# A graph-attention kernel: tiles of x transposed by VectorE in 32x32 blocks, with the features in another order, in place of TensorE

## The chip, the cores and the metric

The kernel runs on one core of a Trainium2 chip. The metric is the device time of one execution in microseconds (us). Timed runs are given as their median; the profile is of one further execution, whose own time is given beside it.

## The reference

There are N = 3327 nodes with D = 512 features, an N x N matrix `adj` of zeros and ones, two weight matrices of 512 x 1024 (one per attention layer) and one of 512 x 512. All is float32.

```
for l in 0, 1:                       # two attention layers
    Wh, Ws = split(x @ W[l])         # each N x 512
    a = softmax(Wh @ Ws.T) * adj     # N x N
    x = leaky_relu(a @ Wh + x)
x = layernorm(x0 + x)
b = max(sign(x), 0)
x = layernorm(x + relu(adj @ (b @ sign(weight).T)))
```

The order of the 512 features is free inside one product that sums over them, as long as both sides use the same order. The change rests on that.

## The kernel before

Rows of x are cut into tiles of 128 (26 tiles, the last with 127 rows), four tiles make a chunk (7 chunks, the last with two tiles), two tiles make a pair. Each layer has two stages: `project`, then `attention`.

**project(l)** makes what attention reads. Its matmuls sum over the features, so the features must lie on the partitions: each chunk of x is needed as `xT`, 128 feature partitions x 4 feature blocks x 512 rows. `load_x(c)` loads the chunk's tiles `xr` by rows (one DMA of 256 KB a tile, on SP's queue). `transpose_x(c, k, lane)` transposes the four tiles' block k on TensorE through PSUM, four instructions (L263), and copies the result to `xT` with one copy by ACT (L268; for chunk 0 by ACT and VectorE in turn, L121 and L123).

From `xT` come three things:

- `keys`: four sums of quarter blocks of `xT` on VectorE (L180 to L183), all stored to DRAM (`xs_d`) by POOL's queue.
- `project_values`: Wh of a pair as a product of Strassen's form, `seven`: seven products (`pZ_wh`, `pX_wh`, `pY_wh`) of the quarters of `xT` with those of `wa` (the first half of W) and with `wsum`, sums of those quarters made by `sums_w` on VectorE. Three PSUM banks, X, Y and Z, hold partial sums. A product that adds to bank Z must wait until ACT has copied out what was there (L159).
- `queries`: the chunk's x times M, in the same form (`pZ_g`, `pX_g`, `pY_g`), where M is the product of the two halves of W (`product_m`, tiles `pm`, matmuls L235). M needs both halves transposed, which `transpose_w` does on TensorE (L213, copies `wTs`). `xt` are sums of quarters of `xT` (L186 to L189), `msum` sums of quarters of M.

In layer 0, M is made at the beginning of `project`. In layer 1 it is made during the last steps of the first attention: `load_w` loads both halves on SP's queue, `transpose_w` and `product_m` are woven between attention's matmuls.

**attention(l)** goes through 13 x 13 steps. SP's queue brings `ws`, `adj`, `xs` and `gs` a few steps ahead; VectorE and ACT make the softmax, POOL sums, TensorE the products of scores and of values. Rows of the next x are finished by VectorE (L790, L793) and stored to `x1_d`.

The order of instructions on each engine is written out by hand: `weave` sorts pieces of several lists by their place in the list, and pieces like the transposes of the next chunk (`turns`) stand between the matmuls of the current one. All small tiles come from one ring of equal slots (`slot`). After layer 1's begin, `binary_weights` loads four tiles `wT` through a ring of two buffers and works on them on VectorE (L464, L466).

Of the kernel before, what the change touches and what calls it, by code (L numbers as in the profile page):

```python
# [19 lines left out]
P = 128  # L20
CT = 4
CW = CT * P
HW = CW // 2
NEG_SLOPE = 0.01
EPS = 1e-5
# [4 lines left out]
def kernel(  # L30
# [21 lines left out]
    def tiles_of(c):  # L52
        return range(c * CT, min(NT, (c + 1) * CT))
# [23 lines left out]
    def slot(shape, dtype, name):  # L77
        return ring.tile(shape, dtype, tag="s", bufs=SBUFS, name=name)
# [32 lines left out]
    def load_rows(eng, dst, src, r):  # L111

        cut = r - r % 16
        if cut:
            eng.dma_start(out=dst[:cut], in_=src[:cut])
        if cut < r:
            eng.dma_start(out=dst[cut:r], in_=src[cut:r])

    def copy_out(n, dst, src):
        if n % 2:  # L120
            nc.scalar.copy(dst, src)  # L121
        else:
            nc.vector.tensor_copy(dst, src)  # L123
# [76 lines left out]
    ch_lane, acc_lane, tr_lane = (ps_ch, "ch"), (ps_acc, "acc"), (ps_tr, "tr")  # L200
    w_rows, wT, m_of, wsum_of = {}, {}, {}, {}

    def load_w(l, h):

        for k in range(KD):
            w_rows[l, h, k] = slot([P, D], F32, f"w{h}_{l}_{k}")
            nc.sync.dma_start(out=w_rows[l, h, k], in_=w_stack[l, ts(k, P), ts(h, D)])

    def transpose_w(l, h, k, lane):
        pool, tag = lane  # L210
# [32 lines left out]
    def project(l, pre):  # L243
# [1 line left out]
        src = x if l == 0 else x1_d  # L245
        xTs, rows_of = {}, {}

        def load_x(c):
            rows_of[c] = []
            for t in tiles_of(c):  # L250
                xt = slot([P, D], F32, f"xr_{l}_{t}")
                load_rows(nc.sync, xt, src[t * P : t * P + rows(t), :], rows(t))
                rows_of[c].append(xt)

        def transpose_x(c, k, lane):
            if k == 0:
                xTs[c] = pre.tile([P, KD, CW], F32, tag="xT", bufs=2, name=f"xT_{l}_{c}")
            pool, tag = lane
            pt = pool.tile([P, CW], F32, tag=tag, name=f"pxt_{l}_{c}_{k}")
            w = 0  # L260
            for a, t in enumerate(tiles_of(c)):
                r = rows(t)
                nc.tensor.transpose(  # L263
                    pt[:, w : w + r], rows_of[c][a][:r, ts(k, P)], ident[:r, :r]
                )
                w += r
            if c:
                nc.scalar.copy(xTs[c][:, k, :w], pt[:, :w])  # L268
            else:
                copy_out(k, xTs[c][:, k, :w], pt[:, :w])  # L270
            n = len(tiles_of(c)) * P
            if w < n:
                nc.gpsimd.memset(xTs[c][:, k, w:n], 0.0)


        load_x(0)
        wa = pre.tile([P, KD, D], F32, tag="wa", bufs=1, name=f"wa_{l}")
        for k in range(KD):
            nc.sync.dma_start(out=wa[:, k], in_=w_stack[l, ts(k, P), :D])
        if l == 0:  # L280
            load_w(l, 1)
            for k in range(KD):
                w_rows[l, 0, k] = wa[:, k]
        load_x(1)
        for k in range(KD):
            transpose_x(0, k, acc_lane)
        if l == 0:
            for h in range(2):
                for k in range(KD):
                    transpose_w(l, h, k, (acc_lane, ch_lane)[h])  # L290
        if l == 0:
            for k in range(2):
                sums_w(l, k)
        wsum = wsum_of[l]
        lo, hi = wa[:, 0:2], wa[:, 2:4]
        wr = {B11: lo[:, :, :HD], B21: hi[:, :, :HD], B22: hi[:, :, HD:]}
        wr.update({i: wsum[:, e] for e, i in enumerate((T1, T2, T3, T4))})
        m = pre.tile([P, KD, D], F32, tag="m", bufs=1, name=f"m_{l}")
        if l == 0:
            m_of[l] = [m[:, 0:2], m[:, 2:4]]  # L300
# [120 lines left out]
        def prepare(c):  # L421
            start, *chains[c] = queries(c, (ch_lane, ch_lane if c else acc_lane))
            if start:
                start()

        if l == 0:
            first, second = (project_values(0, a, ch_lane) for a in range(2))
            weave(product_m(l, acc_lane), first + second, [lambda: prepare(0)])
            sums_m()
        else:  # L430
            first, second = (
                project_values(0, a, lane) for a, lane in enumerate((ch_lane, acc_lane))
            )
            weave(first, second, [sums_m, lambda: prepare(0)])
        for c in range(NC):
            turns = []
            if c + 1 < NC:
                turns = [lambda k=k: transpose_x(c + 1, k, tr_lane) for k in range(KD)]
                pairs_of[c + 1] = project_values(c + 1, 0, acc_lane)
                turns += [pairs_of[c + 1].pop(0), lambda: prepare(c + 1)]  # L440
            turns = rest + turns
            rest = [chains[c][1].pop()] if chains[c][1] else []
            if c + 2 < NC:
                load_x(c + 2)
            if c == 0:
                weave(*chains[c], turns)
            else:
                one, two = chains[c]
                pairs = pairs_of[c]
                for a in range(1, len(tiles_of(c)) // 2):  # L450
                    pairs += project_values(c, a, acc_lane)
                rest.append(pairs.pop())
                weave(one + two, pairs, turns)
# [735 lines left out]
```

## Time and profile before

| | us |
|---|---|
| three timed runs | 2652.05, 2652.95, 2653.69 |
| median | 2652.95 |
| profiled execution, its own time | 2652.55 |
| its span, first to last instruction | 2650.7 |
| TensorE busy | 2614.6 |
| VectorE busy | 2046.3 |
| ACT busy | 812.1 |
| POOL busy | 1091.3 |
| mean share of the 16 DMA engines on SP's queue | 60.4% |

PE is TensorE's matmuls and PEld its weight loads, which overlap them; DVE is VectorE, ACT ScalarE, POOL GpSimd, SP SyncE, and SPq the DMAs that SP issues. A name such as `pxt<-ident,xr` gives the tile written and the tiles read; xN is a count. Matmuls overlap, so that the duration of one is longer than the distance to the next: what a matmul costs TensorE is read from the starts. A float32 product appears as two rows per matmul of the source. In rows in order of time, the first number is the start in us from the span's begin, the second the time from there to the end of the last instruction merged into the row, and the brackets give the idle time before it and what ended it.

### The profile page before, as it was taken

To read this page: it belongs to the slowest core of one execution; us is meant where nothing else is said; L and a number is where in the kernel's file an instruction comes from. 1 tells how busy PE (TensorE), PEld (TensorE's weight loads), DVE (VectorE), ACT (ScalarE), POOL (GpSimd) and SP (SyncE) were. 2 spreads that over 40 slices of the span, in tenths; PEclk is the share of its full clock that TensorE was granted. 3 is DMA by queue.
4 is the path that set the end of the run, shared out by engine and by line. 5 is a ranking of instruction groups with operands and counts; after the bars stand their busy time and mean duration, and the time that the engine had idled before them with its cause. 6 is when DMAs were issued, how large, how long until landed. Compare 5 with 4: busy or idle time off the path is not lost. (4 is left out here: it accounts for less than half of the span.)

```text
span 2650.7 us, 40451 instructions
## 1 busy us (share of the span) xinstructions
PE 2614.6 (99%) x12839; PEld 2271.0 (86%) x12864; DVE 2046.3 (77%) x4211; ACT 812.1 (31%) x2000; POOL 1091.3 (41%) x2029
## 2 busy tenths in 40 slices
PE   9999999999999999999999999999999999999998
PEld 7888888888888888887888888888888888888787
DVE  5554888899888896666754589988899888767976
ACT  3333332333333332221333333333333333222143
POOL 2550343444444444546552044444444444455510
PEclk9999999999999999999999999999999999999999
DMA  5754777777777776776865677777777777677875
GB/s 205 272 193 157 260 239 251 253 266 252 259 244 244 267 248 222 235 245 230 294 219 180 210 231 272 241 257 260 233 270 247 252 255 236 228 260 260 278 245 168
DMA packets 285186, 638.63 MB, mean 241 GB/s; under 512 B 32141, under 2 KB 146671, under 8 KB 283430
## 3 DMA queue, kind: packets, MB, share of 16 engines
q1 hardware_dynamic: 249206, 529.52, 60.4%
q0 software_dynamic: 35760, 106.45, 10.8%
q8 instruction: 105, 1.72, 0.3%
q14 instruction: 115, 0.94, 0.1%
HBM read 528.91 MB, written 106.93 MB: 240 GB/s over the span
## 5 line engine op out<-in xcount | busy, mean ns | idle before, releaser
L500 PE MATMUL pZ<-gs,xs 128*128 128x256 f32 x2496 | 636.2, 379 | 1.7 <-ACT u L517 1.7
L699 POOL TENSOR_TENSOR as<-s 128x128 f32<-128x128 f32 x338 | 163.4, 484 | 1037.0 <-DVE s L661 691.9
L500 PEld LDWEIGHTS pZ<-gs,xs 128*128 128x128 f32 x2496 | 473.3, 190 | 67.8 <-ACT u L517 3.6
L726 PE MATMUL acc<-ws,s 128*128 128x256 f32 x1352 | 402.6, 379 | 0.0
L726 PE MATMUL acc<-wh,s 128*128 128x256 f32 x1352 | 355.9, 379 | 0.0
L726 PE MATMUL acc<-ws,as 128*128 128x256 f32 x1352 | 349.7, 380 | 1.8 <-POOL as L701 1.2
L648 ACT ACTIVATE s<-s 128x512 f32<-128x512 f32 x338 | 213.3, 631 | 377.7 <-DVE s L645 377.1
L500 PE MATMUL pY<-gs,xs 128*128 128x256 f32 x1248 | 320.7, 379 | 2.2 <-ACT p L517 2.2
L726 PEld LDWEIGHTS acc<-ws,as 128*128 128x128 f32 x1352 | 255.2, 190 | 42.3 <-issue 5.8
L726 PEld LDWEIGHTS acc<-wh,s 128*128 128x128 f32 x1352 | 257.3, 190 | 35.2
L726 PEld LDWEIGHTS acc<-ws,s 128*128 128x128 f32 x1352 | 256.2, 190 | 34.4
L570 DVE TENSOR_TENSOR top<-top,s 128x512 f32<-128x512 f32 x312 | 225.4, 735 | 69.0 <-ACT s L557 48.5
L500 PEld LDWEIGHTS pY<-gs,xs 128*128 128x128 f32 x1248 | 236.7, 190 | 36.0 <-ACT p L517 3.8
L645 DVE TENSOR_TENSOR s<-s,off 128x512 f32<-128x512 f32 x338 | 249.2, 737 | 0.1
L661 DVE TENSOR_TENSOR s<-s,adj 128x512 f32<-128x512 f32 x338 | 236.8, 701 | 9.4 <-DMA adj<-in_adjT_dram 1.0
L656 DVE TENSOR_TENSOR total<-total,s 128x512 f32<-128x512 f32 x312 | 231.8, 743 | 0.0
L517 ACT COPY u<-pZ 128x256 f32<-128x256 f32 x312 | 115.8, 371 | 345.5 <-PE pZ L500 344.9
L701 POOL TENSOR_TENSOR as<-s 128x128 f32<-128x128 f32 x338 | 204.7, 606 | 26.5
L726 PE MATMUL acc<-wh,as 128*128 128x256 f32 x676 | 203.0, 382 | 0.0
L700 POOL TENSOR_TENSOR s<-s 128x128 f32<-128x128 f32 x338 | 183.3, 542 | 27.6
L702 POOL TENSOR_TENSOR as<-s,as 128x128 f32<-128x128 f32 x338 | 180.7, 535 | 26.5
L542 DVE TENSOR_TENSOR s<-p,u 128x256 f32<-128x256 f32 x156 | 66.8, 428 | 151.7 <-ACT u L517 151.7
(206 smaller groups left out, 3883.9 us busy)
## 6 DMA issues: line engine op xcount, KB each, us to landing
ws<-ws_d SPq DMA_DIRECT2D x338, 512.0 KB, 3.8
xs<-xs_d SPq DMA_DIRECT2D x182, 512.0 KB, 5.8
adj<-in_adjT_dram SPq DMA_DIRECT2D x324, 256.0 KB, 4.2
xs<-xs_d SPq DMA_DIRECT2D x156, 384.0 KB, 6.5
gs_d<-gsp POOLq DMA_DIRECT2D x88, 256.0 KB, 2.8
gs<-gs_d SPq DMA_DIRECT2D x12, 1792.0 KB, 10.9
adj_d<-ab POOLq DMA_DIRECT2D x169, 112.0 KB, 3.8
ahl<-adj_d SPq DMA_DIRECT2D x78, 224.0 KB, 4.7
```

Of the source, the lines that this page charges most:

```text
L500: nc.tensor.matmul(ch[bank], xs[c, q, a][:, k], gs[c][:, b, k], start=(start and k == 0), stop=(k == 1), skip_group_check=True,)
L517: nc.scalar.copy(ch[name], ch[bank])
L570: nc.vector.tensor_tensor(top[i], top[i], t, ALU.max)
L645: nc.vector.tensor_tensor(s, s, off[g].to_broadcast([P, 2, HW]), ALU.subtract)
L648: nc.scalar.activation(sc[g, q], sc[g, q], AF.Exp)
L656: nc.vector.tensor_tensor(total[g], total[g], sc[g, q], ALU.add)
L661: nc.vector.tensor_tensor(s, s, adj[g, q], ALU.mult)
L699: nc.gpsimd.tensor_tensor(s3, a11, a21, ALU.subtract)
L700: nc.gpsimd.tensor_tensor(a21, a21, a22, ALU.add)
L701: nc.gpsimd.tensor_tensor(s2, a21, a11, ALU.subtract)
L702: nc.gpsimd.tensor_tensor(s4, a12, s2, ALU.subtract)
L726: nc.tensor.matmul(acc[g][i // 2][:, i % 2], a[i], b[i], start=(q == 0 and i % 2 == 0), stop=(q == NQ - 1), skip_group_check=True,)
```

## The change

`load_x` now loads one tile so that its four 128-column blocks lie on four quadrants of 32 partitions: one DMA for each quadrant (`load_laid`), in which partition v of the quadrant gets row v of each of the tile's four groups of 32 rows. `transpose_x` is then one VectorE instruction a tile, which transposes every 32x32 block. No PSUM tile and no copy remain. After it, partition 32a+u of block k holds feature 128a+32k+u, so the rows of both halves of W are loaded in that order too: `load_features` (four DMAs for `wa`, as before) and `load_w` (16 DMAs for a half, before 4). At the begin of each layer's `project`, the DMAs are issued by SP and ACT in turn; everywhere else by SP. The begin is in another order: the first pair's product starts when two tiles and `wa` are there, and the transposes of W follow, woven between its products.

```diff
--- before.py
+++ after.py
@@ -20,6 +20,7 @@
 P = 128
 CT = 4
 CW = CT * P
+B = 32
 HW = CW // 2
 NEG_SLOPE = 0.01
 EPS = 1e-5
@@ -116,6 +117,36 @@
         if cut < r:
             eng.dma_start(out=dst[cut:r], in_=src[cut:r])
+    def load_laid(engines, dst, src, n):
+        full = n // B
+        for a in range(CT):
+            eng = engines[a % len(engines)]
+            if full:
+                eng.dma_start(
+                    out=dst[ts(a, B), :full],
+                    in_=src[: full * B, ts(a, P)].rearrange("(r v) f -> v r f", v=B),
+                )
+            if full * B < n:
+                cut = (n - full * B) // 16 * 16
+                for lo, hi in ((0, cut), (cut, n - full * B)):
+                    if lo < hi:
+                        eng.dma_start(
+                            out=dst[a * B + lo : a * B + hi, full],
+                            in_=src[full * B + lo : full * B + hi, ts(a, P)],
+                        )
+    def load_features(engines, dst, src):
+        for a in range(CT):
+            engines[a % len(engines)].dma_start(
+                out=dst[ts(a, B)], in_=src[ts(a, P)].rearrange("(k u) n -> u k n", u=B)
+            )
     def copy_out(n, dst, src):
         if n % 2:
             nc.scalar.copy(dst, src)
@@ -200,11 +231,15 @@
     ch_lane, acc_lane, tr_lane = (ps_ch, "ch"), (ps_acc, "acc"), (ps_tr, "tr")
     w_rows, wT, m_of, wsum_of = {}, {}, {}, {}
-    def load_w(l, h):
+    def load_w(l, h, engines=(nc.sync,)):
         for k in range(KD):
-            w_rows[l, h, k] = slot([P, D], F32, f"w{h}_{l}_{k}")
-            nc.sync.dma_start(out=w_rows[l, h, k], in_=w_stack[l, ts(k, P), ts(h, D)])
+            wt = w_rows[l, h, k] = slot([P, D], F32, f"w{h}_{l}_{k}")
+            for a in range(CT):
+                row = a * P + k * B
+                engines[a % len(engines)].dma_start(
+                    out=wt[ts(a, B)], in_=w_stack[l, row : row + B, ts(h, D)]
+                )
     def transpose_w(l, h, k, lane):
         pool, tag = lane
@@ -245,56 +280,40 @@
         src = x if l == 0 else x1_d
         xTs, rows_of = {}, {}
-        def load_x(c):
-            rows_of[c] = []
-            for t in tiles_of(c):
-                xt = slot([P, D], F32, f"xr_{l}_{t}")
-                load_rows(nc.sync, xt, src[t * P : t * P + rows(t), :], rows(t))
-                rows_of[c].append(xt)
-
-        def transpose_x(c, k, lane):
-            if k == 0:
+        def load_x(t, engines=(nc.sync,)):
+            xt = rows_of[t] = slot([P, CT, P], F32, f"xr_{l}_{t}")
+            if rows(t) < P:
+                nc.gpsimd.memset(xt[:, CT - 1], 0.0)
+            load_laid(engines, xt, src[t * P : t * P + rows(t), :], rows(t))
+        def transpose_x(t):
+            c, a = divmod(t, CT)
+            if a == 0:
                 xTs[c] = pre.tile([P, KD, CW], F32, tag="xT", bufs=2, name=f"xT_{l}_{c}")
-            pool, tag = lane
-            pt = pool.tile([P, CW], F32, tag=tag, name=f"pxt_{l}_{c}_{k}")
-            w = 0
-            for a, t in enumerate(tiles_of(c)):
-                r = rows(t)
-                nc.tensor.transpose(
-                    pt[:, w : w + r], rows_of[c][a][:r, ts(k, P)], ident[:r, :r]
-                )
-                w += r
-            if c:
-                nc.scalar.copy(xTs[c][:, k, :w], pt[:, :w])
-            else:
-                copy_out(k, xTs[c][:, k, :w], pt[:, :w])
-            n = len(tiles_of(c)) * P
-            if w < n:
-                nc.gpsimd.memset(xTs[c][:, k, w:n], 0.0)
-
-
-        load_x(0)
+            nc.vector.transpose(
+                xTs[c][:, :, ts(a, P)].rearrange("p k (r v) -> p r k v", v=B),
+                rows_of.pop(t).rearrange("p r (k u) -> p r k u", u=B),
+            )
+        begin = tiles_of(0)
+        engines = (nc.sync, nc.scalar)
+        for t in begin[:2]:
+            load_x(t, engines)
         wa = pre.tile([P, KD, D], F32, tag="wa", bufs=1, name=f"wa_{l}")
-        for k in range(KD):
-            nc.sync.dma_start(out=wa[:, k], in_=w_stack[l, ts(k, P), :D])
+        load_features(engines, wa, w_stack[l, :, :D])
+        for t in begin[2:]:
+            load_x(t, engines)
         if l == 0:
-            load_w(l, 1)
+            load_w(l, 1, engines)
             for k in range(KD):
                 w_rows[l, 0, k] = wa[:, k]
-        load_x(1)
-        for k in range(KD):
-            transpose_x(0, k, acc_lane)
-        if l == 0:
-            for h in range(2):
-                for k in range(KD):
-                    transpose_w(l, h, k, (acc_lane, ch_lane)[h])
-        if l == 0:
-            for k in range(2):
-                sums_w(l, k)
-        wsum = wsum_of[l]
+        for t in tiles_of(1):
+            load_x(t)
+        for t in begin[:2]:
+            transpose_x(t)
         lo, hi = wa[:, 0:2], wa[:, 2:4]
         wr = {B11: lo[:, :, :HD], B21: hi[:, :, :HD], B22: hi[:, :, HD:]}
-        wr.update({i: wsum[:, e] for e, i in enumerate((T1, T2, T3, T4))})
         m = pre.tile([P, KD, D], F32, tag="m", bufs=1, name=f"m_{l}")
         if l == 0:
             m_of[l] = [m[:, 0:2], m[:, 2:4]]
@@ -423,25 +442,39 @@
             if start:
                 start()
+        first, second = (
+            project_values(0, a, lane)
+            for a, lane in enumerate((ch_lane, ch_lane if l == 0 else acc_lane))
+        )
+        first.pop(0)()
         if l == 0:
-            first, second = (project_values(0, a, ch_lane) for a in range(2))
-            weave(product_m(l, acc_lane), first + second, [lambda: prepare(0)])
+            for k in range(2):
+                sums_w(l, k)
+        wr.update({i: wsum_of[l][:, e] for e, i in enumerate((T1, T2, T3, T4))})
+        turns = [lambda t=t: transpose_x(t) for t in begin[2:]]
+        if l == 0:
+            wa_turns = [lambda k=k: transpose_w(l, 0, k, tr_lane) for k in range(KD)]
+            weave(first, wa_turns, turns)
+            for k in range(KD):
+                transpose_w(l, 1, k, acc_lane)
+            weave(product_m(l, acc_lane), second, [lambda: prepare(0)])
             sums_m()
         else:
-            first, second = (
-                project_values(0, a, lane) for a, lane in enumerate((ch_lane, acc_lane))
-            )
+            for do in turns:
+                do()
             weave(first, second, [sums_m, lambda: prepare(0)])
         for c in range(NC):
             turns = []
             if c + 1 < NC:
-                turns = [lambda k=k: transpose_x(c + 1, k, tr_lane) for k in range(KD)]
+                turns = [lambda t=t: transpose_x(t) for t in tiles_of(c + 1)]
                 pairs_of[c + 1] = project_values(c + 1, 0, acc_lane)
                 turns += [pairs_of[c + 1].pop(0), lambda: prepare(c + 1)]
             turns = rest + turns
             rest = [chains[c][1].pop()] if chains[c][1] else []
             if c + 2 < NC:
-                load_x(c + 2)
+                for t in tiles_of(c + 2):
+                    load_x(t)
             if c == 0:
                 weave(*chains[c], turns)
             else:
```

## The prediction

> **What bounds the kernel now.** I read the busy shares first, then the list of what TensorE waited for, then the time-ordered view around the two places where a projection begins (us 0 and us 1257).
>
> ```profile
> PE 2614.6 (99%) x12839; PEld 2271.0 (86%) x12864; DVE 2046.3 (77%) x4211; ACT 812.1 (31%) x2000; POOL 1091.3 (41%) x2029
> L263 PE MATMUL pxt<-ident,xr x208: 272/273/476, 3.7 to 1408.0; 128*128 128x128 f32 x104
> 50.00:100.00 50.00, 50.00 (x250) 44.03 (x249) 30.95 (x72) 18.71 (x46) 27.46 (x46) 1.00 0.82 297
> ```
>
> The first line says that TensorE sets the time: 99% busy, and its waits add up to only some 25 us. The second counts the transposes of x: 208 in all (26 tiles, 4 blocks, 2 layers). The third, a window inside the first projection (span, then busy PE, PEld, DVE, ACT, POOL, clock, DMA share, GB/s), shows TensorE full and VectorE at 30.95 of 50 us: what leaves TensorE there is gain, and VectorE has 19 us free.
>
> The price of a transpose isn't its 273 ns, since matmuls overlap. It is read from starts:
>
> ```profile
> 1256.73 0.38 PE L774 MATMUL pz<-ident,total 128*128 128x128 f32 x2
> 1256.95 1.91 PE L263 MATMUL pxt<-ident,xr 128*128 128x128 f32 x16
> 1258.90 1.99 PE L338 MATMUL pZ_wh<-wa,xT 128*128 128x256 f32 x8
> ...
> 1272.53 1.89 PE L394 MATMUL pZ_g<-xT,m 128*128 128x256 f32 x8
> 1274.26 0.60 PE L263 MATMUL pxt<-ident,xr 128*128 128x128 f32 x4
> 1274.69 1.89 PE L394 MATMUL pX_g<-xT,m 128*128 128x256 f32 x8
> ...
> 1277.45 1.99 PE L394 MATMUL pZ_g<-xt,msum 128*128 128x256 f32 x8 [0.43 <-DVE xt L187]
> ```
>
> Four transposes take 1274.26 to 1274.69: 0.108 us each. Eight rows of a product take 1272.53 to 1274.26: 0.216 each, so one Strassen product of `seven` (four rows) is 0.86 us.
>
> [...] No VectorE transpose is in this trace; the price I take is [...] 0.69 us, which the 128x512 copies here agree with (0.68). [...]
>
> **The change, part by part.** The compiled instruction list of the changed kernel shows TensorE with 208 instructions fewer.
>
> *Loops.* 208 less 16 in the first start and 24 around the second leaves 168 x 0.108 = **-18.1 us**. ACT loses 48 copies of 0.585 us and VectorE gains a transpose a tile: about 8 tiles per 50 us x 0.69 = 5.5 us of the 19 free, cost 0. The cover is that slack; it would be gone at about 2.4 us per transpose. POOL gains a memset per layer, also hidden. SP issues four DMAs a tile, 0.45 us each, 1.8 us per tile of 6.3 us, a chunk ahead: 0 (bounds -2 and +3, for x comes in 512 B pieces while the DMA share is 0.57 to 0.82).
>
> *First start.* Before:
>
> ```profile
> 0.74 1.28 ACT L121 ACT_TABLE_LOAD   x1 [0.74 <-PEq L1176]
> 0.75 1.83 SPq L115 DMA_DIRECT2D xr<-in_x_dram  x4
> 2.62 1.85 SPq L279 DMA_DIRECT2D wa<-in_w_stack_dram  x4
> 4.52 2.88 SPq L207 DMA_DIRECT2D w<-in_w_stack_dram  x4
> ```
>
> Products begin at 14, and the first query product `pZ_g` at 39.89. After, 36 DMAs (16 x, 4 wa, 16 w) are split between SP and ACT, and in the compiled list each waits for the one eight before it[...]. So they go in rounds: first pair on each queue at 0.75; those land at about 0.75+2.5 = 3.2 (the shortest landing of an x tile before is 2.6); wa issues at 3.2, 1 MB lands by about 8.3; then x tiles 2 and 3, then w rows at about 2.6 us a round. ACT's sixteenth DMA issues at 13.5, its table load (1.28) comes only then, and its first copy ends at 15.7. TensorE starts earlier, at 8.3, but the second product into bank Z needs that copy, so it stalls from 10.6 to 15.7. From there 5 products (4.3), 12 transposes of wa and 16 of w (3.0) and copies lead to 23.3; 16 `pm` matmuls (0.86 each) and 7 products give 23.3+13.8+6.0 = 43.1. Against 39.5 (`pZ_g` issues its weights then): **+3.7 us** (bounds +1 and +7).
>
> *Second start.* Before, SP loaded x tiles 0 to 3 at 1195.8 to 1199.4 and wa at 1247.2, far ahead. After, half of wa and of tiles 2 and 3 is issued by ACT, in order behind the last copy of M, L121, which ran 1256.07 to 1256.65. So wa lands at about 1260.5, ACT's last x DMAs wait for it and land at about 1263.3. VectorE holds two transposes, the residual work that ended at 1262.3, four sums, then transposes of tiles 2 and 3: 1265.5. The second pair's first product waits for that. 13 more products and 8 rows each of `pZ_g` and `pX_g`: 1265.5+11.2+3.5 = 1280.2. Next needs `xt` from VectorE. VectorE is itself behind `wT`:
>
> ```profile
> 1264.90 8.64 SPq L462 DMA_DIRECT2D wT<-in_weightT_dram  x4
> 1268.63 0.43 DVE L464 TENSOR_SCALAR neg_w<-wT 128x512 bf16<-128x512 f32 x1 [2.83 <-DMA wT<-in_weightT_dram]
> ```
>
> In SP's queue `wT` now comes behind 16 DMAs for tiles 4 to 7, the first of which waits on ACT's DMAs: it issues at about 1268 and lands at 1271.4 to 1273.7. In the changed order all four `wT` stand ahead of the `xt` sums on VectorE, so `xt` comes at 1282.3 to 1285. Against 1277.45: +4.9 to +7.5; I take **+6** (bounds +2 and +12, the first if only the wait for tiles 2 and 3 counts).
>
> *W of layer 1.* 32 DMAs in place of 8 on SP, at 1121 and 1130, where the DMA share is 0.96 and a w DMA took 6.7 us to land. Two batches of 16 x 0.45 = 7.2 us each hold up `ws` loads (issued two 4.75 us steps ahead, landing in 3.8). About at the edge: **+1.2** (0 to 5).
>
> Sum: -18.1+3.7+6+1.2 = **-7.2 us**. The profiled execution took 2652.55 (span 2650.7 and 1.85 around it), so 2645.35; the median of the runs is 0.4 above it: **2645.8**.
>
> **Rivals.**
> *Rounds of small DMAs are longer* (slower). The starts are chains of DMAs: 4 rounds in the first, about 5 in the second. I took 2.6 us a round, but x tiles took 4.4 us at the median, with traffic. At 4.4: 9 x 1.8 = 16, and some 4 more at the w loads: -7.2+20 = +13, 2666. The gain is gone at 3.4 us a round; it is slower by over 0.2% at about 4. For it: DMA share 0.8 and above in such places. Against: at both starts the queues are otherwise nearly empty.
> *The starts cost little* (faster). If ACT's loads land early and VectorE's order gives no wait, +1 and +2 with nothing at the w loads: -15, 2638. For it: before, these starts waited only 1 us on engines. Against: ACT's in-order position, which is certain.
> *VectorE's float32 transpose takes several passes.* [...]the loops still just fit, but ten transposes stand in line at the starts: +16, 2661. That the change doesn't do what it says is excluded by the instruction list.
>
> **How the numbers follow.** A measurement here can tell about 0.2%, 5.3 us. Forecast as summed 0.48, starts cheap 0.22, long rounds 0.22, slow transposes 0.08. The forecast's own spread (+-6) puts part of it within 0.2%. Faster 0.55, same 0.24, slower 0.21. Range 2636 (starts cheap and a little more) to 2662 (most of long rounds).
>
> **What would show it.** Right: no L263 rows; transposes of 0.7 us on VectorE; TensorE's first rows at 8 and a wait for ACT until about 15; a wait of about 8 us near 1245 for wa and for tiles 2 and 3, then one for `xt`; loops with no new waits. Wrong: transposes over 1.5 us, or TensorE waits inside the loops, or `ws` waits after the w loads above 5 us.

## The result and the profile after

The changed kernel takes 2658.59 us (median of 20 runs, 2655.32 to 2660.56) against 2652.43 (20 runs, 2650.38 to 2655.31): a ratio of 1.0022, 95% interval 1.0015 to 1.0029, so 0.22% slower. Its profiled execution took 2658.96 us, its span 2657.2, against 2652.55 and 2650.7 before.

What the change does in the loops came out as forecast. First the page's busy line of the kernel after:

```profile
PE 2602.3 (98%) x12656; PEld 2256.5 (85%) x12656; DVE 2074.0 (78%) x4259; ACT 784.6 (30%) x1948; POOL 1093.9 (41%) x2023
```

The transposes in the answer on the tile xT (min/median/max ns, first and last start), in place of the 208 rows of L263:

```profile
L293 DVE STREAM_TRANSPOSE xT<-xr x52: 667/702/712, 4.1 to 1413.6; 128x512 f32<-128x512 f32 x52
```

The window inside the first projection that was shown of before (span, then busy PE, PEld, DVE, ACT, POOL, clock, DMA share, GB/s):

```profile
50.00:100.00 50.00, 50.00 (x232) 43.82 (x231) 36.60 (x79) 15.74 (x42) 22.34 (x38) 1.00 0.79 282
```

TensorE is busy 12 us less, one VectorE transpose takes 0.702 us, and VectorE's load in this window rises by 5.65 of 50 us and is hidden. Yet the span grew by 6.5 us. Three places took more than the loops gave. The first start, in order of time (start, duration, engine; in brackets the idle time before and what ended it):

```profile
0.74 1.86 ACTq L130 DMA_DIRECT2D xr<-in_x_dram  x4
0.75 1.81 SPq L130 DMA_DIRECT2D xr<-in_x_dram  x4
...
4.62 6.66 ACTq L130 DMA_DIRECT2D xr<-in_x_dram  x4
...
11.19 2.05 PE L357 MATMUL pZ_wh<-wa,xT 128*128 128x256 f32 x4 [11.19 <-DMA wa<-in_w_stack_dram]
...
11.41 6.51 ACTq L240 DMA_DIRECT2D w<-in_w_stack_dram  x8
...
17.95 1.28 ACT L190 ACT_TABLE_LOAD   x1 [17.95 <-DMA w<-in_w_stack_dram]
...
19.67 2.07 PE L357 MATMUL pZ_wh<-wsum,s 128*128 128x256 f32 x4 [3.99 <-ACT h_wh L190]
```

`wa` is there at 11.19. ACT stands behind its own DMAs until 17.95 and loads the table for its activation function only then, and TensorE waits 3.99 us for its first copy. The end of the first attention:

```profile
1120.90 9.86 SPq L240 DMA_DIRECT2D w<-in_w_stack_dram  x16
1130.85 0.37 SPq L740 DMA_DIRECT2D ws<-ws_d  x1
...
1133.26 12.17 SPq L240 DMA_DIRECT2D w<-in_w_stack_dram  x16
...
1140.26 1.10 PE L533 MATMUL pD<-gs,xs 128*128 128x256 f32 x4 [1.83 <-DMA xs<-xs_d]
1145.53 0.37 SPq L740 DMA_DIRECT2D ws<-ws_d  x1
...
1149.35 2.05 PE L759 MATMUL acc<-ws,as 128*128 128x256 f32 x4 [2.81 <-DMA ws<-ws_d]
```

Two bursts of 16 `w` DMAs hold SP's queue for 9.86 and 12.17 us, the next `ws` is issued only after each, and TensorE waits. What SP itself waited for in us 1116 to 1150 (us in total, times, longest) tells why the bursts are that long:

```profile
SPq L240 <- DMA xs<-xs_d: 4.6, 2, 2.6
SPq L240 <- DMA ws<-ws_d: 1.0, 1, 1.0
SPq L240 <- DMA adj<-in_adjT_dram: 1.0, 2, 0.8
```

Within the bursts SP stood 6.6 us for earlier loads to land. The second start:

```profile
1258.15 20.07 SPq L130 DMA_DIRECT2D xr<-x_d  x20
...
1269.16 2.05 PE L357 MATMUL pZ_wh<-wa,xT 128*128 128x256 f32 x4 [3.63 <-DMA wa<-in_w_stack_dram]
...
1272.92 2.04 PE L357 MATMUL pZ_wh<-wa,xT 128*128 128x256 f32 x4 [1.71 <-DVE xT L293]
...
1278.58 9.84 SPq L495 DMA_DIRECT2D wT<-in_weightT_dram  x4
1282.91 0.43 DVE L497 TENSOR_SCALAR neg_w<-wT 128x512 bf16<-128x512 f32 x1 [7.96 <-DMA wT<-in_weightT_dram]
...
1290.18 1.99 PE L413 MATMUL pX_g<-xT,m 128*128 128x256 f32 x8 [1.39 <-DVE wb L193]
...
1293.73 1.97 PE L413 MATMUL pZ_g<-xt,msum 128*128 128x256 f32 x8 [1.55 <-DVE xt L218]
```

TensorE waits for `wa`, for the transposes of tiles 2 and 3, for `wb`, a sum of VectorE, and for `xt`; VectorE itself waited 7.96 us for `wT`. One more thing shows in all three places: four rows of a product take about 2.05 us there, against 1.03 elsewhere. After these waits TensorE ran at half rate for some microseconds. Two windows of the kernel after, the clock third from the end:

```profile
19.00:26.00 7.00, 6.33 (x19) 5.10 (x20) 1.04 (x2) 1.99 (x6) 0.00 (x0) 0.52 0.48 132
1146.00:1156.00 10.00, 7.19 (x21) 5.49 (x20) 3.58 (x7) 1.00 (x2) 2.02 (x5) 0.66 0.94 318
```

The clock stands at 0.52 and 0.66 there, and at 1.00 in the window from 50 to 100. Between the times at which the recorded clock changes, the three stretches at half rate are these:

```profile
18.86:25.67 6.81, 6.00 (x16) 4.84 (x17) 1.04 (x2) 2.08 (x5) 0.00 (x0) 0.50 0.49 134
1148.67:1155.48 6.81, 6.13 (x16) 4.88 (x17) 1.71 (x4) 0.37 (x1) 1.82 (x4) 0.50 1.02 352
1268.14:1278.36 10.22, 7.49 (x17) 5.58 (x18) 6.64 (x14) 2.63 (x4) 7.91 (x13) 0.50 0.83 264
```

In each, half of TensorE's busy time is lost: 3.0, 3.1 and 3.7 us by this estimate. The kernel before runs at the full rate from us 10.9 to 2485.6. The stretches are two and three times 3.41 us, the length of a fourth one in the kernel after (from us 2493.51 on, clock 0.50). A wait of 2.81 us was enough here: the clock fell 2.1 us into it, 2.6 us into the wait of 3.63 and 3.2 us into that of 3.99. What sets these lengths is not shown.

### The profile page after: what moved, and what is told of

The parts are those of the page before. It is cut to its first block, busy times and chain, and to the rows that moved or that the text cites. A ratio compares the mean times of both kernels' runs of the same rounds, so it can differ in the third digit from the quotient of the medians.

```text
span 2657.2 us, 40332 instructions
## 1 busy us (share of the span) xinstructions
PE 2602.3 (98%) x12656; PEld 2256.5 (85%) x12656; DVE 2074.0 (78%) x4259; ACT 784.6 (30%) x1948; POOL 1093.9 (41%) x2023
## 5 line engine op out<-in xcount | busy, mean ns | idle before, releaser
L694 DVE TENSOR_TENSOR s<-s,adj 128x512 f32<-128x512 f32 x338 | 237.2, 702 | 15.7 <-DMA adj<-in_adjT_dram 6.8
```

The source lines that it names most:

```text
L694: nc.vector.tensor_tensor(s, s, adj[g, q], ALU.mult)
```

## The experiments

Five marks on TensorE cut each profiled execution into six parts: the start of the first `pZ_g` on `xT`; from there to the first `pZ` of attention ("loops 0"); to the last `pz` ("attention 0"); to the first `pZ_g` on `xt` ("second start"); to the last `pZ_wh` on `wsum` ("loops 1"); the rest. All in us, from the profiled execution; the ratio is of timed runs to those of before on the same chip.

| run | first pZ_g | loops 0 | attention 0 | second start | loops 1 | rest | span | ratio (95%) |
|---|---|---|---|---|---|---|---|---|
| before | 39.9 | 155.6 | 1061.3 | 20.7 | 150.5 | 1222.8 | 2650.7 | |
| after | 50.4 | 145.9 | 1068.9 | 28.6 | 141.7 | 1221.8 | 2657.2 | 1.0022 (1.0015 to 1.0029) |
| e1_spread_w | 48.8 | 145.9 | 1062.3 | 29.0 | 141.7 | 1222.7 | 2650.3 | 0.9994 (0.9985 to 1.0002) |
| e2_sp_begin | 43.7 | 145.9 | 1067.2 | 24.8 | 141.7 | 1221.6 | 2644.8 | 0.9979 (0.9971 to 0.9987) |
| e3_sp_begin_warm | 46.0 | 145.9 | 1068.4 | 25.9 | 141.7 | 1222.1 | 2650.0 | 0.9984 (0.9978 to 0.9991) |
| e4_before_split_w | 40.3 | 155.6 | 1067.5 | 21.1 | 150.5 | 1222.3 | 2657.2 | 1.0023 (1.0013 to 1.0034) |
| e5_one_w | 49.4 | 145.9 | 1082.2 | 29.0 | 141.7 | 1221.6 | 2669.7 | 1.0063 (1.0049 to 1.0076) |
| e6_one_w_sp | 51.1 | 145.9 | 1081.8 | 24.9 | 141.6 | 1223.2 | 2668.4 | 1.0059 (1.0046 to 1.0073) |
| e7_turns_first | 50.1 | 145.9 | 1081.8 | 24.1 | 141.6 | 1223.7 | 2667.1 | 1.0055 (1.0041 to 1.0069) |
| e8_wa_first | 52.1 | 145.9 | 1078.6 | 24.0 | 141.7 | 1224.0 | 2666.2 | 1.0062 (1.0048 to 1.0076) |
| e9_spread_sp | 44.6 | 145.9 | 1060.9 | 24.7 | 141.6 | 1221.6 | 2639.3 | 0.9952 (0.9938 to 0.9965) |
| e10_big_begin | 43.3 | 145.9 | 1060.2 | 25.0 | 141.6 | 1221.4 | 2637.4 | 0.9947 (0.9933 to 0.9961) |
| e11_big_wa_first | 43.1 | 145.9 | 1060.6 | 25.0 | 141.6 | 1221.4 | 2637.6 | 0.9949 (0.9936 to 0.9963) |
| e12_second_start | 43.5 | 145.9 | 1060.6 | 20.4 | 141.6 | 1223.3 | 2635.3 | 0.9952 (0.9938 to 0.9965) |
| e13_2k_pieces | 42.6 | 145.9 | 1060.6 | 24.7 | 141.6 | 1221.6 | 2637.1 | 0.9945 (0.9930 to 0.9960) |
| e14_big_warm | 40.7 | 145.9 | 1063.0 | 24.9 | 141.7 | 1222.9 | 2639.1 | 0.9946 (0.9933 to 0.9960) |
| e15_warm_defer | 41.4 | 145.9 | 1063.6 | 23.4 | 141.7 | 1221.6 | 2637.6 | 0.9946 (0.9933 to 0.9960) |
| e16_warm_defer_bw | 41.1 | 145.9 | 1062.2 | 22.1 | 141.6 | 1222.7 | 2635.7 | 0.9934 (0.9920 to 0.9947) |
| e17_128_partitions | 41.0 | 145.9 | 1061.0 | 25.2 | 141.6 | 1221.5 | 2636.1 | 0.9935 (0.9920 to 0.9950) |
| e18_defer_bw | 42.9 | 145.9 | 1061.2 | 20.4 | 141.6 | 1222.3 | 2634.3 | 0.9938 (0.9925 to 0.9952) |

Kernels whose first start is the same code differ in that part: after 50.4 and e1 48.8 (by the starts, rows at half rate until us 25.7 and until about 22.8), e2 43.7, e9 44.6 and e12 43.5. So a single difference of about 1 us in it tells nothing.

### W's bursts: undone alone, and done alone

e1, the changed kernel with the bursts spread (`load_w` takes the blocks `ks` it is to load):

```diff
-early[end - 14 + 2 * h] = [(0.9, lambda h=h: load_w(l + 1, h))]
+for k in range(KD):
+    early[end - 14 + KD * h + k] = [(0.9, lambda h=h, k=k: load_w(l + 1, h, ks=(k,)))]
...
```

> The changed kernel, but layer 1's W is loaded four small DMAs a step over eight steps of the first attention instead of in two bursts of sixteen. Burst theory (the two bursts, 9.9 and 12.2 us of SP's queue, hold back the loads of xs and ws, TensorE waits 4.6 us for them and runs at half clock after the longer wait): the waits on xs and ws in us 1140 to 1150 go, the last pz before the second projection comes at about 1257.5 in place of 1265.2, span about 2649.6 in place of 2657.2, median about 2651 (ratio to before 0.9995). Rival A (the number of small DMAs costs, wherever they stand): pz stays within 2 us of 1265, span 2655 to 2657. Rival B (the gain is given back at the second start, because its loads are late by the clock and not by TensorE's place): pz at 1257.5, but the span falls by less than 3 us.

e4, the kernel before with bursts and nothing else:

```diff
-nc.sync.dma_start(out=w_rows[l, h, k], in_=w_stack[l, ts(k, P), ts(h, D)])
+for a in range(CT if l else 1):
+    n = P // CT if l else P
+    nc.sync.dma_start(
+        out=w_rows[l, h, k][ts(a, n)],
+        in_=w_stack[l, k * P + a * n : k * P + (a + 1) * n, ts(h, D)],
+    )
```

> The kernel before, with nothing changed but layer 1's W loads: each DMA of 128 rows is cut into four of 32 rows, so 32 DMAs in two bursts of sixteen in place of eight, same bytes, same layout. Burst theory: TensorE waits for xs and ws near us 1140 to 1150 as in the changed kernel, the last pz before the second projection comes at 1263 to 1265 in place of 1256.7, span about 2657.5 in place of 2650.7, ratio to before about 1.0026. Rival (the lag in the first attention comes from the changed rotation of slots or from DMA traffic of the x pieces, not from the bursts): pz within 2 us of 1256.7, ratio 1.000. A middle value would mean that part of the 7.6 us depends on the changed kernel's other transfers.

Spreading takes 6.6 of attention 0's 7.6 us away; bursts alone in the kernel before add 6.2. Both theories' numbers were met, and the rivals fall: the same small DMAs, spread, leave attention 0 only 1.0 us longer than before. The order of time of e4 shows the same burst and the same wait as in the changed kernel:

```profile
1121.21 9.58 SPq L209 DMA_DIRECT2D w<-in_w_stack_dram  x16
...
1149.17 2.05 PE L731 MATMUL acc<-ws,as 128*128 128x256 f32 x4 [2.79 <-DMA ws<-ws_d]
```

### ACT as an issuer, and the clock

e2 changes one line, `engines = (nc.sync, nc.scalar)` to `(nc.sync,)`.

> The changed kernel, but SP alone issues the DMAs at the begin of each layer's projection. Theory (ACT stands in order behind its DMAs): ACT's table load is at 1 us instead of 17.95, TensorE's 4.0 us wait for ACT's first copy near 19.7 goes, so the first query product pZ_g starts at about 46.4 in place of 50.4; at the second start wa is there before TensorE needs it, so the waits of 3.6 us for wa and 1.7 us for the transposes go; span about 2657.2 - 4 - 5.3 = 2648, and down to 2645 if xt is no longer late because wT is issued earlier. Rival A (rounds of landings alone set the first start, so that the W rows come no earlier and TensorE waits for them instead): pZ_g at 49 to 51. Rival B (at the second start the wait for xt behind wT absorbs whatever is won before it): the lag of the second start stays 6 to 8 us, span about 2653.

The first start fell by 6.6, the second by 3.8 us, and the span to the low end of what was expected. In e2's order of time ACT's first copy follows the first product at once:

```profile
11.71 2.04 PE L357 MATMUL pZ_wh<-wa,xT 128*128 128x256 f32 x4 [11.71 <-DMA wa<-in_w_stack_dram]
...
13.79 0.37 ACT L190 COPY h_wh<-pZ_wh 128x256 f32<-128x256 f32 x1 [11.76 <-PE pZ_wh L357]
```

`wa` is 0.5 us later with one queue (11.71 against 11.19): that is all the second issuing queue had bought here, and it cost ACT's place. The 6.6 is more than the 4.0 of the wait, since without it TensorE did not fall back to half rate in e2 (clock 1.00 in us 18 to 26, against 0.52 in us 19 to 26 after; the four rows of the first `wsum` product took 0.86 us to the next instruction there, 1.87 in after): 4.0 and the 3.0 estimated above, less 0.5, are 6.5.

At the second start not all went as expected. The wait for `wa` (3.63) gave way to one of 1.85, and those for `wb` and `xt` went, but the wait for the transposes of tiles 2 and 3 grew from 1.71 to 4.43 instead of going.

e3 is e2 with work ahead, in layer 0:

```diff
+pwarm = ps_tr.tile([P, CW], F32, tag="tr", name="pwarm")
+for n in range(56):
+    nc.tensor.transpose(pwarm[:, ts(n % CT, P)], ident, ident)
```

> As the kernel with SP alone at the begins, and 56 transposes of the identity on TensorE ahead of the first projection, whose result nobody reads: TensorE is busy from about 1.5 us until about 10 us, shortly before wa lands. Clock theory (after the first 11 us of idleness TensorE runs at half rate until some us of work are done): the first product's four rows take 0.9 us to the next instruction in place of 1.84, the granted clock over us 11 to 26 is near 1.0 in place of 0.77, and the first pZ_g comes 3 to 4 us earlier than with SP alone. Rival A (the slow rate at the start comes from waits of the weight loads or from DMA traffic, not from idleness): the four rows still take about 1.84 us, no gain. Rival B (wa or W land later than TensorE would need them, so the faster clock only lengthens a wait): clock near 1.0, but pZ_g moves by less than 1 us.

The four rows took 0.94 us to the next instruction (11.92 to 12.86), as the clock theory has it, but TensorE then waited 2.0 us for W and the clock fell to 0.53 in us 24 to 26 (the next six rows of `pm` took 3.89 us, against 2.65 in e2). That is rival B's mechanism, and worse than its number: `pZ_g` was 2.3 us later. The gain of warmth alone stayed open until e14.

### Fewer DMAs for W: a miss

```diff
-for a in range(CT):
-    row = a * P + k * B
-    engines[a % len(engines)].dma_start(out=wt[ts(a, B)], in_=w_stack[l, row : row + B, ts(h, D)])
+rows_k = w_stack[l, :, ts(h, D)].rearrange("(a k u) n -> k a u n", a=CT, u=B)[k]
+engines[k % len(engines)].dma_start(out=wt, in_=rows_k)
```

> The changed kernel, but a 128-row tile of W in the new row order is loaded by one DMA (a four-level address pattern) instead of four, in both layers: same bytes, same 2 KB pieces, a quarter of the DMAs. Theory that the number of DMAs in the queues counts: the attention of layer 0 (first pZ to last pz) takes about 1061.5 us in place of 1068.9, as before; in the first start ACT is through its DMAs at about 12 in place of 17.95, so that TensorE's 4.0 us wait for it goes and pZ_g starts at about 45 in place of 50.4; the second start stays 7 to 9 us longer than before. Span 2644 to 2646, ratio to before 0.998. Rival (the scattered rows themselves are slow to move, so fewer DMAs change nothing): attention 0 stays at 1067 to 1069, span 2652 to 2657.

It was 0.63% slower. A window of e5, in the second of W's loads:

```profile
1138.00:1146.00 8.00, 3.87 (x9) 3.19 (x10) 0.69 (x1) 0.09 (x1) 1.81 (x4) 0.62 0.26 99
```

The DMA engines are busy 0.26 and move 99 GB/s while TensorE waits for `ws` (14.0 us in all). What keeps the share so low is not shown. The edit changes the form of the DMAs together with their number (one now takes a tile of W from four blocks of 32 rows), so e5 says nothing on the number of DMAs, and the three kernels built on it are blurred: at the first start they waited for W to land (4.3 us in e6, 4.7 in e8), so that e8's question fell away there.

> W by one DMA a tile, and SP alone issuing at the begins. If the causes are separate they add: attention of layer 0 as before (1061 to 1062.5), pZ_g at 43 to 44, the second start (last pz to the first pZ_g on xt) at 24 to 25 us against 20.7 before, span 2637.5 to 2640, ratio 0.9953. Rival (the waits cover one another, what is won in one place is lost in the next): span 2643 or more.

> As with W by one DMA a tile and SP alone, and in layer 1 the transposes of x tiles 2 and 3 stand ahead of the first product and its sums on VectorE. Theory (TensorE waits 4.4 us for them only because VectorE has residual rows and sums queued ahead of them, and runs at half rate after that wait): the wait for xT goes or falls below 1 us, the second start falls from about 24.7 to 19 to 21 us, span 4 to 6 us below that of the kernel without this. Rival A (the tiles land late, so the order on VectorE is not what holds them): the wait stays at 3 to 5 us. Rival B (xt behind wT becomes the next wait): the wait for xT goes, but the second start falls by less than 2 us.

> As with the transposes first, and in layer 0 wa is loaded ahead of x tiles 0 and 1, and TensorE begins with the 16 transposes of wa, as the kernel before began with x and W. Theory (the first start is bound by how long the first DMAs take: TensorE stands idle until wa is there at 11.7, and the cold clock costs two more): TensorE starts at 5 to 6 us, the cold clock falls on the transposes while x is still on its way, the first pZ_g comes at 40 to 41.5 in place of 43.7, and the span falls by 2 to 3 us. Rival (x's 512-byte pieces, behind wa, now land so late that TensorE waits for xT instead): pZ_g at 43 or later.

Their edits: e6 is e5 with e2's line; e7 adds

```diff
+if l:
+    for t in begin[2:]:
+        transpose_x(t)
 first.pop(0)()
```

and takes these transposes out of their old place in layer 1; e8 issues `load_features` of `wa` ahead of x tiles 0 and 1 in layer 0 and calls `transpose_w(l, 0, k, tr_lane)` for all k ahead of the first product.

e6's sum failed with e5. e7 still tells something: the wait for tiles 2 and 3 fell only from 4.4 to 3.0 and the second start by 0.8. Two residual rows of layer 0 (1280.47 to 1283.2) still stood ahead of their transposes on VectorE, which followed without a gap, so it was not the landing that held them.

### Both repairs together

> Both repairs that worked alone: layer 1's W four small DMAs a step, and SP alone issuing at the begins. If the causes are separate, they add: first pZ_g at 43.5 to 44.5, attention of layer 0 (first pZ to last pz) 1061 to 1062.5 us, second start (last pz to the first pZ_g on xt) 24 to 25, span 2638 to 2640.5, ratio to before 0.9955. Rival (one wait covers another): span 2643 or more.

They add: 0.48% faster than before, and 0.7% than the changed kernel by the two ratios. What is left are 4.7 us at the first start and 4.0 at the second. The largest wait there is the one for tiles 2 and 3:

```profile
1259.14 2.05 PE L357 MATMUL pZ_wh<-wa,xT 128*128 128x256 f32 x4 [4.43 <-DVE xT L293]
```

### The rest of the first start

e10 is e9, but loads x for layer 0's begin in pairs of tiles, and W's second half by four DMAs:

```diff
-    load_x(t, engines)
+    nc.sync.dma_start(
+        out=wide[ts(a, B), ts(p, 2 * CT)],
+        in_=src[ts(p, 2 * P), ts(a, P)].rearrange("(r v) f -> v r f", v=B),
+    )
...
-    load_w(l, 1, engines)
+    load_features(engines, m, w_stack[l, :, D:])
```

(`wide` is the tile that `msum` takes later, `m` that of M.)

> As with both repairs, and at layer 0's begin larger DMAs: x in pairs of tiles (four DMAs of 128 KB a pair, the same 512-byte pieces) and W's second half by four DMAs of 256 KB, so 16 DMAs in place of 36. Theory that SP's issue rate holds the first start (one DMA of 64 KB per 0.46 us is 142 GB/s, and the trace shows 126 to 145 GB/s at half the DMA share from us 2 to 6 with SP alone): DMA share near 1 from us 3 on, wa there at 8.5 to 9.5 in place of 11.7, pZ_g at 41 to 42.3 in place of 43.7. Rival (the 512-byte pieces hold it, whatever the size of a DMA): the rate stays below 200 GB/s while x moves, wa at 11 or later, pZ_g at 43 to 44.5.

The DMA share rose to about 1 (1.05 in us 3 to 10, against 0.49 in us 2 to 6 of e2), but the rate stayed at some 210 GB/s in us 3 to 10 (212, against 209 in e2). `wa` came at 10.6 in place of 11.8, between theory and rival, and `pZ_g` 1.3 us earlier than in e9, little more than kernels of the same first start differ by.

The rival took 512-byte pieces for the cause; e13 changes only them (`src[ts(p, 2 * P), :]` by whole rows). e17 changes the partitions that a DMA fills (`out=wide[:, ...]`, `out=dst[:, a]`), with x in pieces of 1 KB. In both kernels features of layer 0 lie in another order than in W, so that their products are not those of the reference, and only the time is read.

> As with the larger DMAs at layer 0's begin, but the eight DMAs of x there fetch whole rows, pieces of 2 KB in place of 512 bytes, with the same number of DMAs, bytes and quadrants (the features of the first four tiles then lie in another order than W's, so this kernel computes something else for them; only its time is read). Piece theory: in us 3 to 10 the DMA engines move 300 GB/s or more at full share in place of 185 to 230, wa is there at 7.5 to 9 in place of 10.6, the first pZ_g comes 1.5 to 3 us earlier than 43.3. Rival (32-partition destinations or DMAs of 128 KB hold the rate): 185 to 230 GB/s still, pZ_g at 43 to 44.

> As with the larger DMAs at layer 0's begin, the same 16 DMAs in the same order and of the same bytes, but each of those for x, wa and W fills all 128 partitions instead of one quadrant of 32 (x in pieces of 1 KB, features in the order of memory, so that the products of layer 0 are not those of the reference; only the time is read). [...]in us 3 to 10 the rate is 280 GB/s or more, wa is there at 7.5 to 8.8 in place of 10.6, pZ_g comes 1.5 to 2.7 us earlier than 43.3. Rival (the rate at the begin is that of the first microseconds of any kernel): still 185 to 240 GB/s, wa at 10 or later.

The same stretch in e10 (quadrants, mostly pieces of 512 bytes):

```profile
7.00:11.00 4.00, 0.41 (x1) 0.44 (x2) 1.64 (x5) 0.00 (x0) 3.54 (x6) 1.00 1.12 203
```

in e13 (quadrants, 2 KB):

```profile
7.00:11.00 4.00, 0.88 (x2) 0.82 (x3) 1.82 (x6) 0.00 (x0) 3.24 (x5) 1.00 1.07 222
```

and in e17 (128 partitions, x in 1 KB pieces):

```profile
7.00:11.00 4.00, 3.56 (x10) 2.31 (x10) 2.52 (x8) 0.37 (x1) 1.70 (x3) 1.00 1.03 377
```

All three are at full share, but e17's 377 are not loads alone. Its DMAs of this stretch by queue (packets, MB, share):

```profile
q1 hardware_dynamic: 874, 1.07, 76.0%
q0 software_dynamic: 155, 0.44, 27.3%
```

The second line are POOL's stores, which e10 and e13 have none of here. The loads move 1.07 MB in 0.76 of the engines' time, 352 GB/s at full share by estimate. The kernel before, which loads 128 partitions in pieces of 2 KB in this stretch and stores nothing, confirms it:

```profile
7.00:11.00 4.00, 3.90 (x19) 3.91 (x20) 1.38 (x2) 1.17 (x2) 0.87 (x1) 1.00 1.02 368
```

So the partitions made most of the difference here (222 to 368 is 0.60) and the pieces 9% (203 to 222). Why loads into 32 partitions were slower is not shown. The first start fell by 2.4 us, as expected; part of that is that in e17 the first product needs only two of `wa`'s four DMAs (it starts at 6.14). All of `wa` was there by 9.5, which is 1.1 earlier than in e10 and later than the 7.5 to 8.8 expected. e13's first start is 0.7 below e10's, within what equal kernels differ by.

e11 is e10 with `load_features` of `wa` ahead of x, and `transpose_w` of all of `wa` ahead of the first product.

> As with the larger DMAs, and wa is loaded ahead of x, with TensorE's 16 transposes of wa first. If TensorE's idle begin and cold clock are what is left of the first start: TensorE starts at 6 to 8, pZ_g at 39 to 40.5 (the kernel before: 39.9), span 2 us below that of the larger DMAs alone. Rival (x, now behind wa, comes so late that TensorE waits after the transposes, and cools again): pZ_g no earlier than with x first.

TensorE started at 8.0, but its 16 transposes ran at half rate (3.73 us, against 1.91 for 16 later ones in e10) and x came behind them at 12.2. Only 0.3 us were won, nothing that tells. The wait that the rival named was 0.46 us.

e14 is e10 with e3's 56 transposes.

> As with the larger DMAs, and 56 transposes of the identity ahead of the first projection keep TensorE busy until about 10.5 us. Here TensorE does not wait for W later, so that the clock theory can show: the first eight rows take 0.22 us each in place of 0.44, the cold rows between us 10.6 and 16.5 cost 2.5 us less, pZ_g at 40.5 to 41.3 in place of 43.3, span 2 to 2.7 us less. Rival (the slow rows are not from idleness, or a wait for W takes the gain, as with small DMAs): pZ_g at 42.8 or later.

Warmth alone: TensorE's first rows in e14,

```profile
10.24 1.10 PE L378 MATMUL pZ_wh<-wa,xT 128*128 128x256 f32 x4 [0.97 <-DMA wa<-in_w_stack_dram]
11.17 0.60 PE L248 MATMUL pwT<-ident,wa 128*128 128x128 f32 x4
```

against e10,

```profile
10.60 2.05 PE L374 MATMUL pZ_wh<-wa,xT 128*128 128x256 f32 x4 [10.60 <-DMA wa<-in_w_stack_dram]
12.43 1.06 PE L248 MATMUL pwT<-ident,wa 128*128 128x128 f32 x4
```

0.93 us from start to start in place of 1.83, and `pZ_g` 2.6 us earlier: the clock theory's number. The span did not follow. Attention 0 took 2.8 us longer, in small waits for ACT and VectorE (6.2 us in place of 4.5 in that part), and the timed median was 2638.63 against 2638.97. That the warm-up caused these waits is not shown: in kernels without it they add up to 5.0 us (e18), 5.4 (before) and 6.2 (e1) as well.

### The rest of the second start

e12 is e9, and moves two things in VectorE's queue. The residual rows wait in a list that `project(1)` empties behind four transposes:

```diff
-            for do in later:
-                do()
+            later[0]()
+            later[2]()
+            residue.extend((later[1], later[4]))
...
-        if last:
-            binary_weights()
...
+            if last and v == -LOOK:
+                work += [(0.99, binary_weights)]
```

> As with both repairs, and around the second start two pieces of VectorE's queue are moved: the last two residual rows of layer 0 stand behind the transposes of x tiles 0 to 3 instead of ahead of tiles 2 and 3, and binary_weights with its four wT loads is moved into the second attention. Theory (the second start is longer because VectorE, in order, does other work ahead of the transposes and of xt): the wait for xT falls from 4.4 us to below 1.5, no wait for xt, second start 19 to 21.5 us in place of 24.7, span 3 to 5 us below that with both repairs. Rival (tiles 2 and 3 land late; nothing on VectorE matters): the wait for xT stays at 3 us or more, span within 1.5 us.

The wait for tiles 2 and 3 fell from 4.4 to 0.2, there was none for `xt`, as in e9, and the second start is 20.4 (20.7 in the kernel before). Four rows of a product run at full rate:

```profile
1252.27 1.10 PE L357 MATMUL pZ_wh<-wa,xT 128*128 128x256 f32 x4 [1.86 <-issue]
...
1253.57 1.10 PE L357 MATMUL pZ_wh<-wa,xT 128*128 128x256 f32 x4 [0.19 <-DVE xT L293]
```

The timed median, 2640.24 (2637.12 to 2642.17), is hardly below e9's 2640.63, and the profiled execution was the fastest of its five. So e12 shows the gain at its place, not in the whole.

e15 is e14 with e12's first move, e16 with both, e18 is e16 without the warm-up.

> As with warm-up and larger DMAs, and at the second start the two residual rows of layer 0 behind the transposes of tiles 0 to 3 (binary_weights left where it was). If VectorE's order there makes the 4 us: second start 20 to 21.5 in place of 25, median about 2632.5, ratio 0.9925. Rival (with wT's work still ahead of xt, xt is the next wait): second start 23 to 25, median about 2636.5.

> The same with binary_weights moved into the second attention. If its four loads and eight VectorE instructions are hidden there: as the kernel without this move or 1 us faster. Rival (they delay the attention's own loads or VectorE's sums, which in the earlier run cost 1.6 us in a wait of TensorE for s): second start 20 to 21, but the part after it 1 to 3 us longer, median 1 to 2 us above the kernel without this move.

> The larger DMAs at the begin, the residual rows behind the transposes, and binary_weights in the second attention, without the warm-up. The warm-up's 2.6 us at the first start were given back during the attention of layer 0 (1063.0 us in place of 1060.2). If that happens whenever it is there, this kernel is as fast as with it: median 2635.5 to 2637.5, first start 43.3, attention 0 at 1060.5. Rival (the give-back was chance): 2 us slower than with it, 2638.5 to 2639.5.

With the residual rows alone moved (e15) the second start is 23.4, as its rival had it: 0.94 us of wait for `wb`, 1.62 for `xt` behind `wT`, and 3.41 us at half rate (from 1255.86 on eight rows took 2.91 us, against 1.73). With `binary_weights` moved as well these two waits are gone, and it is 22.1 in e16 (again 3.41 us at half rate: clock 0.93 in us 1250 to 1260 and in 1260 to 1275) and 20.4 in e18 (none: 1.00 in both). Both moves are needed. In the timed runs e15 gains nothing on e14 (2639.29 against 2638.63, its rival had 2636.5), e16 2.0 us. e18 beats both kernels: 2636.12 us, 0.62% less than before. The gain of the warm-up, which it lacks, is not to be seen in the timed runs (e16: 2636.62).

## Why the prediction was wrong, point by point

| term | predicted | measured | what made it |
|---|---|---|---|
| loops | -18.1 | -18.5 | right: 0.108 us per transpose removed, VectorE's hidden |
| first start | +3.7 | +10.5 | ACT's place and half rate: 6.6 (e2); loads into 32 partitions: up to 2.4 (e17, with an earlier first product); the rest open |
| W of layer 1 | +1.2 | +7.6 | the bursts: 6.2 to 6.6 (e4, e1); in after 4.6 of waits and 3.1 of half-rate rows |
| second start | +6 | +7.9 | ACT 3.8 (e2), VectorE's order 4.3 (e9 to e12), half rate in both |
| the rest | 0 | -1.0 | not followed up |
| sum | -7.2 | +6.5 | |

The forecast was 7.2 us less and the span grew by 6.5. Two steps made nearly all of these 13.7 us: the timing of the DMA rounds at the first start (6.8 too little) and the length of W's two bursts (6.4 too little). In both, TensorE's half rate after a wait was no term of the sum.

- **Loops.** Price and cover held. The 0.69 us for a transpose was the author's estimate, near VectorE's copies of that size (0.68); 0.702 was measured.
- **First start.** The step that failed is the timing of the rounds: "wa issues at 3.2, 1 MB lands by about 8.3" and "about 2.6 us a round". `wa` was issued at 3.09 and 3.36, but came at 11.19, and ACT's eight `w` DMAs took 6.51 us, so that its last DMA went out at 17.9, not 13.5. The round was taken from the landing of a tile of 128 partitions, while every new DMA fills 32; that accounts for part of it (`wa` 1.1 us earlier in e17 than in e10), and what makes the rest of `wa`'s 2.9 us stays open. ACT's position, its late table load and TensorE's stall on bank Z were foreseen, with the copy's end at 15.7 in place of 19.6. The upper bound, +7, was below the result because the half rate was missing: 3.0 us after the stall by the estimate above, and about 2 more in the first rows, which ran at half rate as well (11.19 to 15.4; four rows took 1.84 us).
- **W of layer 1.** "Two batches of 16 x 0.45 = 7.2 us each ... About at the edge" failed by its size: the bursts took 9.86 and 12.17 us, since SP had to wait 6.6 us within them for earlier loads to land. TensorE's waits were 1.83 + 2.81 = 4.6, within the bound of 5, and 3.1 more went in half-rate rows after the second, which the bound left out.
- **Second start.** ACT in order behind L121, tiles 2 and 3 late, then `xt` behind `wT`: each part was there, and +7.9 lies within the bounds. That the size fits is partly luck. Foreseen were a wait of about 8 us for `wa` and tiles 2 and 3 and one of 2.1 to 4.8 for `xt`. Measured were 3.63 + 1.71 + 1.39 + 1.55 = 8.3 in all, and 3.7 us of half-rate rows, which were not foreseen, made up for the difference.
- **The rival "rounds of small DMAs are longer"** was right that the rounds are longer and named the places, with +13 in all where +6.5 was measured. Their being small is not the cause at the w loads: spread, the same DMAs cost about 1 us (e1).

Not settled: whether the warm-up or chance made the longer attention of e14 to e16, and where the rest's -1.0 comes from. How much of e17's 2.4 us is due to the partitions and how much to the earlier first product was not separated, beyond the 1.1 us by which all of `wa` came earlier.

## What to carry to other kernels

Work taken off the bound engine is worth its price only where the loads that feed the new form come as early as the old ones: price the starts and the queue's bursts with the new shapes (partitions per DMA, DMAs per step), not with landing times of the old. Compare a burst on a queue with the lead of the loads behind it: here bursts of 9.86 and 12.17 us stood ahead of `ws` loads issued two steps of 4.75 us early, and the same DMAs spread over the steps cost about 1 us. And TensorE's waits of 2.8 to 4.4 us cost more than themselves in most of these traces: half-rate rows came after them, 1.7 to 3.7 us.

## What the runs showed of the hardware that was not expected

- In us 7 to 11, loads into 32 partitions moved 203 to 222 GB/s at full share (e10, e13), into 128 partitions 368 (before; e17's 377 contain stores). Pieces of 2 KB (222) were 9% faster than mostly pieces of 512 bytes (203).
- With one DMA for a tile of W from four blocks of 32 rows, the DMA engines stood at a share of 0.26 and 99 GB/s in us 1138 to 1146 (e5).
- One wait of 2.93 us, TensorE's for `ba` before `pbt` late in the kernel, stands in before and after, and one of 2.9 in e9 to e12, e14 to e16 and e18. The recorded clock then fell to half for 3.41 us in before and after. In us 2450 to 2500 it stands at 0.97 in these two, e9 and e10, at 0.93 in e14 and at 1.00 in e16. At the second start a wait of 1.85 us and one of 0.19 were followed by half rate in e15 (eight rows in 2.91 us) and not in e12 and e18 (1.73). So the same wait was followed by half rate in one execution and not in another.
- The traces hold no clock record before the first change to full rate (15.44 us in after, 16.04 in e2), and a window there prints 1.00. In us 11 to 14 of e2 it does, while four rows took 1.83 us (11.71 to 13.54): early on, the starts tell the rate. From TensorE's first row to the full rate it took 4.25 us in after (11.19 to 15.44) and 5.8 in e10 (10.60 to 16.4).
- VectorE's float32 transpose of 32x32 blocks took about as long as its copy of the same size: 0.702 us for 128x512, output scattered, against 0.69 for `wTs` in the kernel before.
